# A two-layer decoder on one core: its planner prices PE's turns between parts of the array, and three groups of instructions become single pieces

## The chip, the cores and the metric

The kernel runs on one core of a Trainium2 chip. The metric is the time of one execution in microseconds (us) on the device; several executions are timed and their median is given. One more execution was taken by the hardware profiler. The engines are called PE (TensorE, matrix products and transposes), DVE (VectorE), ACT (ScalarE), POOL (GpSimd) and SP (the queue that starts most transfers).

## The reference

The input x has 128 sequences of 64 tokens with 128 features, all float32; ctx has the same shape. Two layers follow each other, each with three parts that are added to x after a layer norm:

```python
x = x + L0_attn(ln(x))            # 16 heads of 8, scores times exp(-|decay| * distance), softmax
x = x + L0_xattn(ln(x), ctx, mask)# 16 query heads on 4 key heads of 8, causal and padding mask, norm, Wo
x = x + L0_ffn(ln(x))             # 8 experts, top 2, at most 256 slots an expert are needed here
x = x + L1_attn(ln(x))            # 16 heads of 64, rotary embedding, causal softmax
x = x + L1_xattn(ln(x), ctx)      # bidirectional attention, four parts through W_l
x = x + L1_ffn(ln(x))             # 8 experts, top 1, hidden 512, gelu
```

## The kernel before

The 8192 tokens are cut into 16 supertiles of 512 tokens, each of four tiles of 128 tokens (two sequences a tile). X stays on the chip for the whole program. There are three phases, and each is recorded first and issued afterwards. Phase one walks the 16 supertiles through the first layer's self-attention, cross-attention and routing, and then the eight experts. Phase two walks them through the second layer's two attentions and its routing. Phase three runs 23 blocks of 512 rows through the second mixture of experts.

**The recorder and the planner.** `Loom` records every call as an `Op`: its engine, the views that it reads and writes, and an estimated cost (`effort`). Matmuls that follow each other into the same tile are joined into one op up to a cost of 1.29; `burst()` joins everything inside it into one PE op. An op is issued whole. Each recorded op gets a due time: its supertile's number times a period (`PER0`, `PER_E`, `PER1`, `PER2`) plus a phase from a list (`PHASES0`, `PHASES_E`, `PHASES1`, `PHASES2`), one entry for each op of a supertile. `plan()` sorts each engine's ops by due time and issues in that order; across engines it picks the op that could start first by its own clock of costs, and gives tiles their buffers and banks of PSUM on the way. So the phases set each engine's order, and the costs set which buffer a tile gets and how the engines' streams stand to each other. The planner already has a model of PE's clock (half rate after a window with little work), of the time in which instructions are fetched, and of the loading of activation tables. It has no term for PE going from one part of its array to another.

**Where the change sits.** Matmuls use the whole array of 128 rows by 128 columns or a part of it: the profile shows that as rows*columns. In phase one, `scores8` (L841, 32*64) makes scores, DVE scales or masks them (L930, L957) and takes the maximum (L847), POOL subtracts it (L848), `mixed8` transposes (L858, 128*128) and takes the exponential on ACT (L859), and then multiplies with the values (L868, 128*32) and with ones for the denominators (L875, 128*32); DVE divides (L879, L880). For each of the two tiles t of a call, `mixed8` records three PE ops: L868 for each of two sequences b and L875 once. L938 projects the output; L963 to L972 are the norm after cross-attention, L974 its variance on DVE. L804, L812 and L823 make queries, keys and values, L670 transposes the normed input.

In phase two, L1101 makes rotated queries and keys (DVE L1106, POOL L1109), L1120 the values, `scores64` the scores (L1136, 32*64) in one burst of 16 matmuls for each pair of tile t and head group m, and then for each of two halves i:

```python
for r in range(16):
    l.scalar.activation(rws[:, r, :], rws[:, r, :], AF.Exp, bias=mx[:, r:r + 1])
```

These 16 exponentials (L1146) are 16 separate ops of ACT, each with a due time of its own, so that other work of ACT may be put between them. `mixed64` transposes (L1160), copies (ACT L1161), multiplies with the values (L1169, 64*64), copies (ACT L1172, tile ots) and projects (L1175). The cross-attention after it has L1219, L1229, L1231, the transposes L1249, their copy on ACT (L1251, tile aT), L1262, L1270 and L1277.

Of the kernel before, what the change touches and what calls it, by code (L numbers as in the profile page):

```python
# [20 lines left out]
P = 128  # L21
S = 64
# [33 lines left out]
    17.44, -7.67, -0.70, 53.45, 48.54, 54.04, 45.63, 64.44, 88.63, 76.70, 85.96, 92.76, 172.77, 172.81, 162.05,  # L56
    172.78, 213.44, 234.93, 252.99, 269.10, 251.77, 267.83, 275.66, 267.71, 272.94, 257.68, 279.82, 278.83, 282.38,
    290.67, 293.04, 295.12, 295.46, 292.99, 296.71, 298.01, 298.42, 295.71, 298.60, 321.52, 295.79, 317.71, 306.66,
    305.94, 302.79, 303.43, 299.74, 301.78, 315.30, 316.81, 303.50, 329.32, 300.88, 323.27, 313.42, 317.58, 311.21,
    304.81, 305.08, 309.92, 317.64, 318.35, 306.20, 319.41, 320.24, 224.77, 252.61, 284.62, 298.75, 298.46, 297.40,  # L60
    299.11, 295.06, 316.85, 317.41, 276.24, 277.47, 325.19, 321.67, 321.86, 321.61, 327.96, 323.61, 323.96, 325.67,
    321.37, 324.49, 325.17, 327.24, 343.90, 347.34, 345.14, 340.60, 333.26, 348.22, 333.77, 355.36, 335.28, 342.90,
    343.98, 342.86, 343.43, 344.55, 346.09, 339.00, 351.60, 353.97, 347.01, 351.89, 354.86, 349.07, 349.93, 369.59,
    355.36, 373.48, 360.29, 369.71, 358.54, 368.69, 368.31, 359.10, 359.75, 368.64, 359.10, 373.88, 359.44, 374.41,
    371.20, 361.71, 361.46, 368.84, 366.56, 364.57, 368.59, 368.66, 373.75, 372.93, 386.89, 373.33, 373.42, 376.38,
    374.65, 377.76, 378.07, 377.78, 377.83, 382.39, 378.61, 382.46, 378.24, 382.5, 384.48, 384.54, 383.63, 381.68,
    379.30, 382.10, 386.18, 409.43, 406.59, 406.95, 406.30, 388.81, 391.65, 411.79, 398.09, 398.67, 401.96, 402.84,
    400.64, 403.77, 408.24, 408.65, 401.03, 408.25, 410.28, 411.47, 411.72, 415.13, 410.22, 415.89, 417.95, 419.56,
    444.39, 417.49, 417.41, 402.57, 428.64, 430.52, 432.99, 427.77, 437.23, 426.02, 434.32, 428.63, 434.83, 435.45,
    433.68, 436.02, 437.13, 438.02, 435.47, 434.08, 440.62, 439.70, 440.59, 455.31, 451.94, 447.95]  # L70
PHASES_E = [
    105.53, 216.96, 215.15, 217.11, 217.09, 217.12, 215.52, 107.48, 109.15, 176.01, 219.45, 106.60, 106.75, 175.45,
    217.56, 110.30, 223.67, 207.78, 222.32, 207.78]
PHASES1 = [
    -20.46, 145.81, 193.06, 195.35, 190.35, 171.30, 213.16, 200.50, 220.31, 210.13, 269.78, 283.10, 283.77, 297.78,
    320.65, 312.95, 304.84, 307.46, 338.28, 356.60, 362.19, 357.00, 356.94, 376.04, 344.33, 342.81, 342.61, 365.87,
    364.14, 359.49, 359.01, 380.76, 359.61, 354.22, 354.32, 372.13, 367.75, 361.90, 361.55, 381.69, 375.74, 371.74,
    371.82, 386.79, 381.12, 376.55, 376.18, 393.17, 384.39, 383.56, 391.73, 396.69, 439.67, 396.26, 403.73, 407.54,
    400.11, 396.37, 397.66, 402.37, 398.95, 397.16, 406.48, 430.61, 428.34, 428.16, 425.48, 414.54, 413.96, 420.18,
    429.59, 415.08, 415.07, 430.54, 427.36, 416.03, 422.46, 420.81, 425.31, 420.28, 422.64, 438.57, 398.93, 406.93,  # L80
    428.19, 419.49, 421.08, 417.61, 420.05, 420.04, 425.44, 426.95, 423.91, 437.89, 435.04, 424.61, 421.20, 420.57,
    429.88, 429.72, 421.62, 425.18, 438.82, 425.42, 427.01, 436.31, 436.67, 447.61, 441.7, 455.56, 445.97, 448.47,
    448.42, 413.95, 425.06, 432.86, 435.50, 446.42, 443.68, 466.58, 455.91, 464.02, 456.37, 434.04, 430.56, 429.21,
    429.77, 429.50, 431.19, 430.81, 427.54, 427.18, 429.84, 463.30, 465.33, 459.12, 458.15, 453.17, 466.35, 461.44,
    461.75, 461.06, 461.50, 465.34, 453.43, 449.87, 465.70, 465.01, 452.34, 450.68, 450.88, 457.41, 427.85, 428.57,
    454.82, 461.54, 458.53, 460.45, 462.36, 460.59, 448.56, 459.39, 453.92, 456.75, 455.84, 450.57, 461.14, 449.79,
    451.31, 463.76, 449.52, 449.54, 453.67, 442.24, 441.88, 458.89, 462.62, 466.97, 466.67, 467.98, 469.81, 470.19,
    464.54, 442.43, 442.93, 464.75, 464.67, 467.68, 469.90, 476.72, 470.79, 471.75, 465.75, 424.77, 432.67, 461.49,
    463.46, 466.01, 466.26, 465.36, 466.99, 467.10, 467.15, 485.07, 482.06, 485.04, 488.89, 495.16, 495.96, 489.08,
    496.00, 484.32, 496.66, 497.12, 486.51, 481.07, 499.30, 498.28, 499.42, 497.73, 490.36, 481.95, 482.47, 494.00,  # L90
    484.87, 486.64, 488.98, 511.36, 496.17, 497.35, 498.24, 491.71, 500.93, 499.07, 500.86, 492.13, 506.66, 497.31,
    505.28, 504.50, 495.57, 504.35, 509.70, 515.94, 506.02, 516.41, 506.09, 508.35, 509.21, 508.68, 511.88, 510.84,
    513.64, 510.15, 520.41, 516.91, 523.53, 527.86, 532.29, 533.30, 530.00, 532.06, 525.14, 536.09, 527.96, 521.61,
    523.47, 524.76, 524.75, 522.83, 528.14, 527.96, 526.58, 526.98, 529.26, 542.38, 530.39, 503.68, 533.08, 533.33,
    531.50, 544.83, 534.17, 540.35, 534.65, 537.12, 539.29, 540.66, 541.37, 539.43, 543.70, 545.67, 547.09, 548.20,
    551.06, 553.93, 548.17, 544.84, 552.03, 546.78, 559.80, 561.39, 559.95, 556.15]
# [128 lines left out]
class Op:  # L225
    def __init__(self, index, engine, table):
        self.index, self.engine, self.table = index, engine, table
        self.runs, self.uses, self.into = [], [], None
        self.cost, self.delay, self.count = 0.0, 0.0, 0
        self.needs, self.then, self.waits, self.ready = set(), [], 0, 0.0  # L230
        self.rows = False
# [53 lines left out]
class Loom:  # L285
# [13 lines left out]
    @contextmanager  # L299
    def burst(self):  # L300

        self.bursting = Op(len(self.ops), "PE", None)
        self._add(self.bursting)
        yield
        self.bursting = None
# [16 lines left out]
    def op(self, engine, run, reads, writes, cost, delay=0.05, tables=(), table=None, count=0):  # L322
# [14 lines left out]
        op.rows = engine == "POOL" and bool(tables)  # L337
        op.delay = delay
# [24 lines left out]
    def plan(self):  # L363
# [5 lines left out]
        loaded, count, since, clock = None, 0, 0.0, Clock()  # L369
        order = []  # L370
        while len(order) < len(self.ops):
            best = None
            for e, ops in queues.items():
                for op in ops[:1] if e != "SP" else ops[:40]:
# [3 lines left out]
                    if op.table is not None and op.table != loaded:  # L378
                        t += 1.3
                    if op.count and count + op.count > BLOCK:  # L380
                        t = max(t, since + FETCH)
# [29 lines left out]
            busy[op.engine] = op.many or op.rows  # L411
            end = free[op.engine] + op.delay
# [20 lines left out]
WINDOW, LITTLE = 3.413, 1.5  # L433

# [10 lines left out]
class Recorder:  # L445
# [5 lines left out]
    def __getattr__(self, what):  # L451
        def record(*a, **k):
# [11 lines left out]
            cost, delay = effort(self.engine, what, out, (*a, *k.values()))  # L464
            table = next((x for x in a if isinstance(x, AF) and x in (AF.Exp, AF.Silu, AF.Gelu)), None) if self.engine == "ACT" else None
            count = 0 if self.engine != "PE" else 2 if what == "transpose" else 4
            self.loom.op(self.engine, run, ins, [out] if isinstance(out, View) else [], cost, delay, table=table, count=count)
# [14 lines left out]
def effort(engine, what, out, args):  # L482
# [4 lines left out]
    if engine == "PE":  # L487
        passes = 1 if what == "transpose" else 2
        rows, cols = aps[0].shape[0], out.shape[0]
        share = 1  # L490
        for k in (rows, cols):
            share *= next(x for x in (32, 64, 128) if k <= x) / P
        return passes * max(0.008, (max(cols, n) * 0.00084 + 0.003) * share * 1.02), 0.38
# [22 lines left out]
def decoder_kernel(ctx: ExitStack, tc: tile.TileContext, x, cx, mask, consts, cols, rows, wa, wffn, wouts,  # L516
# [214 lines left out]
    with ExitStack() as ph:  # L731
# [119 lines left out]
        def mixed8(oT, pt, vbd, u):  # L851
# [9 lines left out]
            for t in range(2):  # L861
                pts = both[:, t]
                for b in range(2):
                    h = slice(b * S, (b + 1) * S)
                    with l.burst():
# [6 lines left out]
                with l.burst():  # L872
# [195 lines left out]
    with ExitStack() as ph:  # L1068
# [56 lines left out]
        def scores64(u, qr, kr):  # L1125

            scs = [ps.tile([P, 2, 2, 4, S], F32, name="sc") for i in range(2)]
            for t in range(2):
                for m in range(4):
                    with l.burst():  # L1130
                        for o in range(2):
                            for h in range(4):
                                for b in range(2):
                                    k0 = (2 * u + t) * P + b * S
                                    r = slice(32 * h, 32 * h + 32)
                                    l.tensor.matmul(scs[h // 2][b * S:(b + 1) * S, h % 2, t, m, :], lhsT=qr[r, m, o, k0:k0 + S],  # L1136
                                                    rhs=kr[r, m, o, k0:k0 + S], start=(o == 0), stop=(o == 1))
            pts = []
            for i in range(2):
# [5 lines left out]
                for r in range(16):  # L1145
                    l.scalar.activation(rws[:, r, :], rws[:, r, :], AF.Exp, bias=mx[:, r:r + 1])  # L1146
# [325 lines left out]
```

## Time and profile before

| what | value |
|---|---|
| median of 6 runs | 2085.39 us (2081.73 to 2088.47) |
| profiled execution | 2076.73 us, its span 2075.0 us |
| mean granted PE clock | 0.936 |
| busy share: PE, DVE, ACT, POOL | 87%, 66%, 51%, 63% |
| first layer's attentions | about 0 to 782 us |
| its experts and the way to the second layer | about 782 to 876 us |
| second layer's attentions | about 876 to 1866 us |
| second mixture of experts | about 1866 to 2075 us |

A line of a timeline has the start and the length in us, the engine, the source line, the operation, what it writes and reads, shapes, the count of equal instructions that were merged, and in brackets the idle time of the engine before it with what ended that wait. For PE the shape rows*columns is the part of the array. Each float32 matmul of the program stands as two records, each transpose as one. A list of windows gives for each stretch the busy time and count of PE, PEld (weight loads), DVE, ACT and POOL, the granted PE clock, the share of DMA engines busy, and GB/s.

### The profile page before, as it was taken

Reading aid. Unit: us, or ns where it says so; the run is one execution under the profiler, and the core shown is the slowest. Engines: PE = TensorE matmul, PEld = TensorE weight load, DVE = VectorE, ACT = ScalarE, POOL = GpSimd, SP = SyncE. Lnnn points to the kernel's source line nnn. Section 1 sums busy time; section 2 is a strip of 40 time slices with the busy share of each in tenths; the row PEclk is TensorE's granted clock in tenths of the full one; section 3 lists DMA queues with packets and bytes.
Section 4 is the critical chain, followed back from the end, with each engine's and each line's share of the span. In section 5 each row is a group of like instructions: output and inputs, shape, how many; then the busy total and the mean of one; then the engine's idle time right before and its main releaser. Section 6 shows DMA issues by size and latency. Waiting matters only on the chain. (4 is left out here: it accounts for less than half of the span.)

```text
span 2075.0 us, 67398 instructions
## 1 busy us (share of the span) xinstructions
PE 1798.0 (87%) x29088; PEld 1272.6 (61%) x29088; DVE 1374.2 (66%) x3425; ACT 1054.7 (51%) x2353; POOL 1309.1 (63%) x1184
## 2 busy tenths in 40 slices
PE   5788888888888873489999999999999999839997
PEld 3556566566565652346766766666666666637776
DVE  4767777787777763397777778788777777432222
ACT  5545555455545431136666656676566666613332
POOL 4446667677666665586676676776666666324665
PEclk9988999899999876799999999999999999969999
DMA  3311121111103000601011110100000000014441
GB/s 105 111 45 56 53 58 40 30 36 53 31 25 111 2 2 20 144 12 18 13 28 28 28 28 18 28 22 16 18 15 18 17 18 18 12 62 152 169 170 49
DMA packets 96690, 97.55 MB, mean 47 GB/s; under 512 B 19564, under 2 KB 82372, under 8 KB 96264
## 3 DMA queue, kind: packets, MB, share of 16 engines
q1 hardware_dynamic: 77848, 56.37, 9.3%
q0 software_dynamic: 18544, 36.87, 6.7%
q8 instruction: 228, 3.74, 0.8%
q14 instruction: 70, 0.57, 0.1%
HBM read 56.73 MB, written 45.81 MB: 49 GB/s over the span
## 5 line engine op out<-in xcount | busy, mean ns | idle before, releaser
L1106 DVE TENSOR_TENSOR hv<-ps,cst 128x1024 f32<-128x1024 f32 x256 | 304.8, 1214 | 43.7 <-PE ps L1101 41.1
L1109 POOL TENSOR_TENSOR rot<-hv 128x1024 f32<-128x1024 f32 x128 | 307.3, 2445 | 19.6 <-DVE hv L1106 14.4
L848 POOL TENSOR_TENSOR pt<-pt,mx 128x2048 f32<-128x2048 f32 x64 | 231.9, 3624 | 76.1 <-DVE mx L847 41.6
L1146 ACT ACTIVATE pt<-pt,mx 128x64 f32<-128x64 f32 x1024 | 269.6, 337 | 4.4 <-DVE mx L1144 4.4
L1101 PE MATMUL ps<-xT,w 128*128 128x512 f32 x512 | 252.0, 619 | 7.4 <-ACT ots L1172 6.8
L859 ACT ACTIVATE pts<-ps 128x1024 f32<-128x1024 f32 x128 | 130.4, 1022 | 128.0 <-PE ps L858 100.1
L815 ACT ACTIVATE km<-ps,kb,cst 128x512 f32<-128x512 f32 x128 | 95.7, 779 | 155.9 <-PE ps L670 76.4
L659 POOL TENSOR_SCALAR rs<-mv 128x4 f32<-128x4 f32 x96 | 22.0, 229 | 229.3 <-DVE mv L655 219.8
L638 POOL DMA_INDIRECT xin<-r,slots x128 | 129.7, 1013 | 38.9 <-issue 32.4
L1161 ACT COPY pts<-ps 128x1024 f32<-128x1024 f32 x64 | 64.8, 1014 | 171.4 <-PE ps L1160 170.3
L858 PE MATMUL ps<-ident,pt 128*128 128x128 f32 x1024 | 141.8, 286 | 10.7 <-POOL pt L848 7.4
L1175 PE MATMUL ps<-wo,ots 128*128 128x128 f32 x1024 | 143.3, 284 | 4.0 <-ACT ots L1172 3.5
L847 DVE TENSOR_REDUCE mx<-pt 128x32 f32<-128x2048 f32 x64 | 145.3, 2271 | 0.1
L1175 PEld LDWEIGHTS ps<-wo,ots 128*128 128x128 f32 x1024 | 125.4, 192 | 28.1 <-issue 14.4
L663 ACT ACTIVATE xn<-X,nb,rs 128x128 f32<-128x128 f32 x256 | 114.7, 485 | 53.2 <-POOL nb L661 30.9
L1101 PEld LDWEIGHTS ps<-xT,w 128*128 128x128 f32 x512 | 89.6, 193 | 82.7 <-issue 68.0
L1120 PE MATMUL ps<-w,xT 128*64 128x512 f32 x512 | 134.2, 602 | 0.7 <-DVE hv L1106 0.7
L858 PEld LDWEIGHTS ps<-ident,pt 128*128 128x128 f32 x1024 | 115.5, 146 | 28.5 <-issue 12.3
L1150 POOL TENSOR_TENSOR pt<-pt,den 128x1024 f32<-128x1024 f32 x64 | 120.7, 1907 | 15.7 <-DVE den L1149 12.0
L879 DVE RECIPROCAL rd<-ps 128x256 f32<-128x256 f32 x64 | 112.2, 1753 | 21.7 <-PE ps L868 17.4
L1368 ACT ACTIVATE hT<-ps,wt 128x512 f32<-128x512 f32 x92 | 61.0, 686 | 127.0 <-PE ps L1367 73.8
L1136 PEld LDWEIGHTS ps<-rot,rot 32*64 32x64 f32 x8192 | 96.6, 131 | 41.1 <-ACT vl L1122 12.9
(259 smaller groups left out, 4052.2 us busy)
## 6 DMA issues: line engine op xcount, KB each, us to landing
xsort<-none SPq DMA_DIRECT2D x23, 516.0 KB, 6.3
xe<-xsort SPq DMA_DIRECT2D x23, 516.0 KB, 3.5
ytk<-zero SPq DMA_DIRECT2D x16, 512.0 KB, 3.8
X<-ytk POOLq DMA_DIRECT2D x32, 256.0 KB, 4.7
X<-in_x SPq DMA_DIRECT2D x16, 256.0 KB, 4.8
c<-in_cx SPq DMA_DIRECT2D x16, 256.0 KB, 4.6
c<-in_cx SPq DMA_DIRECT2D x64, 64.0 KB, 2.3
mk<-in_mask SPq DMA_DIRECT2D x16, 128.0 KB, 2.8
```

Source lines behind the costliest of these rows:

```text
L638: i = nc.gpsimd.indirect_dma_start(out=dst, out_offset=bass.IndirectOffsetOnAxis(ap=index.real(), axis=0), in_=src.real(), in_offset=None, ...
L847: l.vector.tensor_reduce(mx, rws, AX.X, ALU.max)
L848: l.gpsimd.tensor_tensor(out=rws, in0=rws, in1=last(mx, S), op=ALU.subtract)
L858: l.tensor.transpose(tp[:, c, :], pt[:, c // 2, t, j0:j0 + 2].rearrange("p j k -> p (j k)"), ident)
L859: l.scalar.activation(both[:, t], tp, AF.Exp)
L1101: l.tensor.matmul(pp[:, h], lhsT=w1[:, qk, c * P:(c + 1) * P], rhs=xT, start=True, stop=True)
L1106: l.vector.tensor_tensor(hv[:, o].rearrange("p h (b s) -> p h b s", s=S), pp.rearrange("p h (b s) -> p h b s", s=S), tab.unsqueeze(2).to_b ...
L1109: l.gpsimd.tensor_tensor(out=r[:, m], in0=hv[:, :, 0], in1=hv[:, :, 1], op=ALU.add)
L1120: l.tensor.matmul(pv[par * S:(par + 1) * S, b], lhsT=xT[:, k0:k0 + S], rhs=w1[:, 2, par * NCH * S:(par + 1) * NCH * S], start=True, stop=True)
L1146: l.scalar.activation(rws[:, r, :], rws[:, r, :], AF.Exp, bias=mx[:, r:r + 1])
L1150: l.gpsimd.tensor_tensor(out=rws, in0=rws, in1=last(den, S), op=ALU.mult)
L1175: l.tensor.matmul(py, lhsT=ots[:, c // 4, c % 4, :], rhs=wo[:, c, :], start=(c == 0), stop=(c == NCH - 1))
```

## The change

The planner's ops get a field `part`, the rows and columns of the array that a PE op uses. When the next PE op has another part than the one before, its start is put 0.095 us after the end of the one before, at the least. The smallest cost of a matmul pass rises from 0.008 to 0.0085. `burst` takes an engine and an activation table. Three groups become single ops: in `mixed8` the L868 matmuls of both sequences and the L875 matmuls of a tile (24 matmuls, before three ops); in `scores64` the scores of two head groups (32 matmuls, before two ops of 16); and the 16 exponentials of a half (before 16 ops of ACT). The lists `PHASES0`, `PHASES_E` and `PHASES1` have new values, with fewer entries where ops were joined; the periods and `PHASES2` are as before. The matmuls and the other arithmetic are the same.

```diff
@@ Loom
-    def burst(self):
-        self.bursting = Op(len(self.ops), "PE", None)
+    def burst(self, engine="PE", table=None):
+        self.bursting = Op(len(self.ops), engine, table)
...
+        op.part = part
@@ plan
+                    if op.part != part and e == "PE":
+                        t = max(t, free[e] + CHANGE)
...
+            part = op.part if op.engine == "PE" else part
...
+CHANGE = 0.095
@@ Recorder
+            part = None
+            if self.engine == "PE":
+                part = next(x for x in (*a, *k.values()) if hasattr(x, "shape") and x is not out).shape[0], out.shape[0]
@@ effort
-        return passes * max(0.008, (max(cols, n) * 0.00084 + 0.003) * share * 1.02), 0.38
+        return passes * max(0.0085, (max(cols, n) * 0.00084 + 0.003) * share * 1.02), 0.38
@@ mixed8
-                for b in range(2):
-                    h = slice(b * S, (b + 1) * S)
-                    with l.burst():
+                with l.burst():
+                    for b in range(2):
+                        h = slice(b * S, (b + 1) * S)
                         for a in range(2):
                             for g in range(4):
                                 l.tensor.matmul(po[32 * g:32 * g + 32, 0, t, h],
...
-                with l.burst():
                     for a in range(2):
                         for g in range(4):
                             l.tensor.matmul(po[32 * g:32 * g + 32, 1, t, :],
@@ scores64
-                for m in range(4):
+                for i in range(2):
                     with l.burst():
-                        for o in range(2):
-                            for h in range(4):
-                                for b in range(2):
+                        for m, o, h, b in product((2 * i, 2 * i + 1), range(2), range(4), range(2)):
...
-                for r in range(16):
-                    l.scalar.activation(rws[:, r, :], rws[:, r, :], AF.Exp, bias=mx[:, r:r + 1])
+                with l.burst("ACT", AF.Exp):
+                    for r in range(16):
+                        l.scalar.activation(rws[:, r, :], rws[:, r, :], AF.Exp, bias=mx[:, r:r + 1])
@@ PHASES0, PHASES_E, PHASES1: all values new
```

## The prediction

> **What bounds the kernel now.** First the stretches: busy time per engine over windows cut at the stages (first layer's attention, its tail with the eight experts, second layer's ramp, steady part and end, the last mixture of experts). Columns: window, its length, then busy us of PE, PEld, DVE, ACT and POOL, granted clock, DMA share, GB/s.
>
> ```profile
> 136.10:426.70 290.60, 247.41 (x4224) 171.78 (x4225) 213.84 (x543) 147.37 (x241) 185.11 (x175) 0.88 0.17 48
> 426.70:737.90 311.20, 269.54 (x4879) 191.82 (x4878) 242.96 (x585) 159.84 (x255) 212.49 (x189) 0.94 0.14 38
> 737.90:874.20 136.30, 68.14 (x684) 49.86 (x683) 56.08 (x263) 23.39 (x48) 74.97 (x87) 0.71 0.25 55
> 976.30:1729.40 753.10, 739.18 (x13535) 512.56 (x13534) 581.57 (x1391) 476.30 (x1297) 523.01 (x435) 1.00 0.09 21
> ```
>
> The second layer (976 to 1729) is TensorE's: 98% busy at clock 1.00, a supertile every 57.8 us (start of L1231, from one to the next). The first layer is not: PE 85 to 87%, DVE 74 to 78%, each waiting for the other, at clock 0.88 and 0.94. The start of L938 comes 47.8 us apart in most of the first eight supertiles and 44.4 in the next five.
>
> Second, PE's timeline in the second layer: start, us, instruction, idle before it.
>
> ```profile
> 1209.46 0.38 PE L1249 MATMUL ps<-ident,a 128*128 128x128 f32 x2
> 1210.31 1.11 PE L1262 MATMUL ps<-aT,c 64*128 64x64 f32 x16 [0.46 <-ACT aT L1251]
> ...
> 1225.86 0.70 PE L1101 MATMUL ps<-xT,w 128*128 128x512 f32 x1 [0.51 <-ACT ots L1172]
> ...
> 1230.06 1.50 PE L1175 MATMUL ps<-wo,ots 128*128 128x128 f32 x12
> 1231.49 0.31 PE L1136 MATMUL ps<-rot,rot 32*64 32x64 f32 x8
> ...
> 1245.89 1.50 PE L1175 MATMUL ps<-wo,ots 128*128 128x128 f32 x12
> 1247.23 0.60 PE L670 MATMUL ps<-ident,r 128*128 128x128 f32 x4
> ```
>
> The same twelve matmuls of L1175 hold PE 1.34 us when the next tile has their part of the array (128*128) and 1.43 us when it is 32*64: entering another part costs 0.09. Leaving a small part costs about as much or more. In the first layer:
>
> ```profile
> 516.50 0.43 PE L868 MATMUL ps<-pts,vbd 128*32 128x64 f32 x16
> 516.75 0.62 PE L875 MATMUL ps<-pts,vone 128*32 128x128 f32 x16
> 517.18 0.41 PE L868 MATMUL ps<-pts,vbd 128*32 128x64 f32 x16
> 517.52 1.12 PE L841 MATMUL ps<-km,qT 32*64 32x256 f32 x32
> ...
> 521.09 1.80 PE L868 MATMUL ps<-pts,vbd 128*32 128x64 f32 x96 [0.82 <-DVE rd L879]
> 523.74 1.13 PE L812 MATMUL ps<-xT,w 128*128 128x512 f32 x2 [0.85 <-DVE oT L880]
> ```
>
> Sixteen of L868 take 0.25 us ahead of L875 (same part) and 0.34 ahead of L841 (another): 0.09 again. Elsewhere (553.37, L868 ahead of L858) it is 0.37 against 0.25, a surplus of 0.12; across the pairs of such rows it runs from 0.09 to 0.14, in a few 0.20. I take 0.11 us a turn, a middle of the common ones.
>
> Third, windows around the waits of the first layer show the clock:
>
> ```profile
> 284.70:289.30 4.60, 1.85 (x98) 1.47 (x97) 2.60 (x6) 3.92 (x7) 4.00 (x7) 1.00 0.03 5
> 289.30:292.80 3.50, 3.50 (x4) 1.11 (x4) 2.67 (x6) 0.00 (x0) 2.07 (x3) 0.51 0.02 6
> ...
> 528.50:531.70 3.20, 1.96 (x36) 1.01 (x36) 2.35 (x4) 0.00 (x0) 1.04 (x1) 1.00 0.01 3
> 531.70:535.10 3.40, 3.33 (x7) 1.51 (x6) 3.40 (x10) 2.03 (x4) 3.32 (x2) 0.50 0.01 0
> ```
>
> After a thin stretch (1.85 busy of 4.6 us) comes one of 3.4 us at half clock. A 47.8 us supertile has about 10.2 us at half clock, a 44.4 us one 3.4; the difference of the two periods is itself one such stretch.
>
> **The change, part by part.** All sums stand against the profiled execution, 2076.7 us (span 2075.0 and 1.7 around it); the median of the six runs is 2085.4, 8.7 higher, which I add at the end. No arithmetic is added or removed: both built programs have 15,646 matmuls. What moves is order, and the order of the built programs is known without a run.
>
> Turns. The changes of part on PE fall from 981 to 847: 496 to 368 in the first layer (32 to 23 a supertile, since L868 and L875 of one tile now stand in one piece of 24), 484 to 478 in the second (31 to 30; the scores, in pieces of 32 instead of 16, were mostly back to back already). So 128 x 0.11 = 14 us, and 6 x 0.11 = 0.7. A turn saved just ahead of a wait is worth nothing. PE's waits in a 44.4 us supertile (the list of waits, 515.5 to 560) sum to 5.5 us, 12%, so I take 88% of 14.7: **-13**. Bounds 0 (every saved turn lies ahead of a wait for DVE) and -18 (0.14 each).
>
> Two waits of the second layer. Now L1262 follows the transposes of L1249 at once and waits 0.46 for ScalarE's copy. In the new order eight matmuls of the output projection (0.22 each) and a pair of L1101 (1.72) stand between: 3.5 us of work over a copy that takes 0.37. It goes, with 0.53 us on PE: 15 x 0.53 = **-8**. L1101's 0.51 is for a bank that the copy ots frees, behind five exponentials. Whether that goes depends on ScalarE: between 0 and -8, I take **-4**.
>
> Exponentials in one piece. Before, 64 sets of 16 are cut up by copies; after, each set is one row of 16. Thirteen in a row took 3.21 us, so a set holds ScalarE 3.9 us, four sets a supertile. Behind each stand, in ScalarE's new queue, copies of ots, vl or pts, whose readers and whose banks' next users are PE's. ScalarE is 63% busy there and has one idle stretch of 8.9 us a supertile, so there is room to place the sets; whether each copy still comes in time the trace of before cannot show. Bounds: 0 for a set that meets slack, and 1.0 us on PE (twice the wait on ots above) for one that does not. I take **0**, the row nearest being L1146's own: 4.4 us of waiting in all, and PE's list of waits in a steady supertile having only the two named.
>
> Waits and clock of the first layer. The longest in a steady supertile are L841 on L974's chain (1.2), L875 and L868 on the reciprocal L879 (1.0 and 0.8), L812 on L880 (0.8). The new order takes L812 from between them and puts it behind the second scores, and the two pairs of L804, which stood together and followed a slow bank, now stand apart with scores and transposes between. The order L963, L967, L969, L972, L841 stays, so the 1.2 us wait and one half-clock stretch probably stay too. I take half a us a supertile, **-8**; bounds -40 (half of all 5.5 us, since DVE with 35 us of work in 44.4 cannot follow much closer) and +30 (a new wait of 1.9, the largest in these rows, in each).
> The early supertiles carry 6.8 us more at half clock, which costs half of it, 3.4, six times: 20 us. In the new build PE's order is the same from the third supertile to the thirteenth, and so it was before; what differed before was VectorE's and POOL's order. I take half: **-10**, bounds 0 and -20.
>
> On that clock the Trainium skill ("TensorE: Matmul & The Clock Gate", section "Why this matters for your kernels") says that matmul bursts keep the full rate as long as PE has no idle gap over about 3 us. The rows speak against it: half clock follows stretches whose longest wait is about 2 us. By the rule there would be no such loss to win back, and the sum would be 10 us smaller.
>
> Ramp, experts, end. The experts' order is new inside each expert (the next expert's transposes move ahead of L1049), but the stretch 738 to 874 is ruled by scatters, the DMA that brings rows back and one 22 us wait for the sums into X, none of which changes; the last stage keeps its phases. **0**, bounds -10 and +10: the phases put the second layer's first work elsewhere, and the 33 us ramp is all waits.
>
> Sum: -13 -8 -4 +0 -8 -10 = -43. 2076.7 - 43 = 2033.7, and with 8.7, **2042**.
>
> **The rivals.**
> ScalarE's pieces decide (slower). If each of the four sets delays a copy that PE needs by the upper bound of 1.0 us, the second layer loses 4 x 16 = 64 us against my 43: 2106. It decides from 43 / 64 = 0.67 us a set. For it: L1101 waits 0.51 already behind a run of only five. Against: the 8.9 us of idle ScalarE.
> The first layer stays at its period. If its waits and half-clock stretches take up the saved turns, as two periods one clock stretch apart suggest, only the 12 us of the second layer come: 2073.
> The first layer loses a clock stretch everywhere: 45.5 us on average falls to 41.0, 15 x 4.5 = 68, and the second layer wins its 12 to 16: about 2003. For it: 1.0 us of turns and 5.5 of waits to win; against: DVE's 35 us of work in strict turn.
> It does nothing: the turns fall, but new waits replace them one for one, 2085. The second layer's one turn in 31 shows how little a merged piece may do.
>
> **How the numbers follow.** Forecast 0.50 (2015 to 2065), first layer stuck 0.17, a stretch gone 0.13, nothing 0.05, ScalarE's pieces 0.15. A difference under 0.2% (4 us) can hardly be told from none here. Faster 0.80, same 0.05, slower 0.15. The range 2004 to 2088 takes in all but the pieces' case and half of the 2003 one.
>
> **What would show it.** Right: L1231 about 56.9 us apart instead of 57.8, L1262 without idle before it, clock 1.00 there; in the first layer L938 43 us apart and the clock above 0.93 from 136 on; L868 to L875 without a turn. Wrong: PE waiting for L1172, L1122 or L1161 in the second layer (pieces); a 44.4 us period kept with more waits on L879 (stuck); a longer gap between the last L1056 and the first L1101.

## The result, and the profile after

The changed kernel took 2091.8 us (median of 28 runs) against 2081.7 (65 runs) for the kernel before: ratio 1.0045, 95% interval 1.0033 to 1.0056, slower by 0.45%. In a later set it was 1.0056 (1.0036 to 1.0075). The prediction was 2042 us, 2004 to 2088, with 0.80 on faster. In three of the sets of experiments below the kernel before itself took 2230 us; ratios are therefore compared only inside a set.

The profiled execution after has a span of 2094.7 us, 19.7 longer than before; the medians are 10 apart, because the profiled execution before lies 5 us under its median (2076.7 against 2081.7) and the one after 5 us over (2096.7 against 2091.8). The shares that follow are of the 19.7. From first rows to first rows: the first layer, from its first L963 to its last (L965 after), fell from 683.2 to 659.9 us; from there to the first L1229 (L1230 after) it is 5.7 us longer; the second layer, from the first of these rows to the sixteenth, rose from 845.9 to 877.3; the end is 4.1 longer, the beginning 1.8. So -23 in the first layer, where about -30 was forecast, and +31 in the second, where -13 was.

First, windows of the profile after: first layer in two parts, then nine supertiles of the second layer and three later ones (columns as before: length, busy of PE, PEld, DVE, ACT, POOL, clock, DMA share, GB/s).

```profile
142.70:426.70 284.00, 244.83 (x4290) 175.28 (x4292) 219.86 (x551) 151.36 (x248) 192.43 (x182) 0.89 0.19 53
426.70:724.50 297.80, 253.29 (x4780) 186.32 (x4774) 234.72 (x573) 152.82 (x239) 202.10 (x182) 0.92 0.13 36
960.30:1514.40 554.10, 525.99 (x9363) 362.97 (x9363) 408.88 (x972) 330.41 (x900) 367.51 (x307) 0.97 0.10 21
1577.50:1751.00 173.50, 170.36 (x3126) 119.28 (x3124) 135.10 (x318) 110.22 (x301) 117.74 (x96) 1.00 0.06 16
```

The third row holds the work of nine supertiles (9,363 matmul records), for which the kernel before took 521 us (9,370 records from 976.1 to 1497.0, PE busy for 511.5, clock 1.00). Here it is 554, PE is 95% busy instead of 98%, and its clock is 0.97. The fourth row is back at 98% and 1.00. Between starts of L1230 the periods are 59.2, then 61.7 to 63.3 eight times, 59.3, and then 57.9, 57.7, 58.0: the loss has a beginning and an end.

Second, PE's waits in the second layer (total, times, longest), before from 976 to 1497 and after from 1019.7 to 1456.3:

```profile
PE ps L1101 <- ACT ots L1172: 4.7, 9, 0.5
PE ps L1262 <- ACT aT L1251: 4.1, 9, 0.5
```

```profile
PE ps L1230 <- DVE lim L1317: 20.6, 8, 2.6
PE ps L1122 <- ACT s L1266: 6.2, 7, 0.9
```

The two waits that the prediction wanted gone, L1262 for aT and L1101 for ots, are gone. Two others stand in their place. (Lines moved by one to three: L1230 is L1229 before, L1122, which makes the values, is L1120, and the copy L1266 is L1265.) The larger one in PE's timeline, and what DVE was doing:

```profile
1143.31 0.58 PE L1230 MATMUL ps<-ident,nmx 128*4 128x128 f32 x2 [2.57 <-DVE lim L1317]
1143.69 1.91 PE L1232 MATMUL ps<-xT,nwc 128*4 128x128 f32 x8
1145.53 2.37 PE L1103 MATMUL ps<-xT,w 128*128 128x512 f32 x4
```

```profile
1137.24 0.42 DVE L1223 TENSOR_REDUCE nmx<-ps 128x4 f32<-128x256 f32 x1
...
1143.00 0.17 DVE L1317 SCALAR_TENSOR_TENSOR lim<-ps,lim 128x8 f32<-128x8 f32 x1
```

L1230 multiplies nmx, which L1223 had ready at 1137.7. PE came to it at 1140.7 and started at 1143.3, at the end of L1317. L1317 updates the routing's limits and has nothing to do with nmx or with what L1230 writes.

Why it waits can be read in the build. The kernel's `BankPool` hands out single banks of PSUM, but what the program knows as a tile is a pair of banks, [128, 1024]. L1230 writes the tile pm in one bank of a pair; the other bank holds the routing's `board`, which L1317 reads. The program places waits by whole tile and by the order in which instructions were issued: an instruction waits for all that touched its pair and was issued earlier, whichever bank it was. In supertiles 2 to 10 of the changed build the last user of the other bank issued ahead of L1230 is L1317, in 11 to 15 it is L1302, some 3.5 us earlier on DVE; in the build before it is L1295 (L1296 after) in every steady supertile. That is one false wait (for work that the instruction doesn't need) in nine supertiles, and the trace shows it nine times.

The stall costs more than its 2.57 us, as three windows around it show:

```profile
1139.00:1143.30 4.30, 1.74 (x59) 1.45 (x49) 3.33 (x14) 3.90 (x7) 2.44 (x3) 0.96 0.06 10
1143.30:1146.70 3.40, 3.39 (x12) 1.81 (x13) 1.02 (x5) 0.22 (x1) 0.38 (x1) 0.55 0.50 70
1146.70:1151.00 4.30, 4.30 (x21) 2.65 (x20) 2.95 (x12) 1.50 (x6) 2.91 (x3) 1.00 0.15 55
```

With 1.74 us of work in 4.3, the next 3.4 us run at about half clock, 1.7 us lost. A period therefore adds up: 57.8 before, less 1.0 for the two waits gone, less 0.1 for one turn, plus 0.9 (L1122), plus 2.57 and 1.7, is 61.9; the trace has 61.7 to 63.3. Two further profiles of the changed kernel (in the second and fourth set below) have the wait nine times each. Three of these 18 waits are not followed by half clock, and their periods are 60.3 and 60.4 us: 1.6 less, the price of the half clock.

The Trainium skill ("TensorE: Matmul & The Clock Gate", section "Why this matters for your kernels") asks for no PE idle gap over about 3 us between bursts. The single gap here is 2.57 us, and the half clock comes after 24 of 27 of them all the same; the measurement decides.

### The profile page after: what moved, and what is told of

It is laid out like the page before. It is cut to its first block, busy times and chain, and to the rows that moved or that the text cites. A ratio compares the mean times of both kernels' runs of the same rounds, so it can differ in the third digit from the quotient of the medians.

```text
span 2094.7 us, 67469 instructions
## 1 busy us (share of the span) xinstructions
PE 1807.3 (86%) x29088; PEld 1288.7 (62%) x29088; DVE 1379.3 (66%) x3425; ACT 1058.3 (51%) x2353; POOL 1308.5 (62%) x1184
## 5 line engine op out<-in xcount | busy, mean ns | idle before, releaser
L1111 POOL TENSOR_TENSOR rot<-hv 128x1024 f32<-128x1024 f32 x128 | 302.1, 2368 | 48.8 <-DVE hv L1108 26.5
L1103 PE MATMUL ps<-xT,w 128*128 128x512 f32 x512 | 259.4, 639 | 0.7 <-ACT xT L1193 0.7
L1147 ACT ACTIVATE pt<-pt,mx 128x64 f32<-128x64 f32 x1024 | 251.2, 337 | 0.4 <-DVE mx L1144 0.4
L641 POOL DMA_INDIRECT xin<-r,slots x128 | 128.4, 1003 | 57.7 <-issue 30.6
L1122 PE MATMUL ps<-w,xT 128*64 128x512 f32 x512 | 140.3, 604 | 11.1 <-ACT s L1266 11.1
L1103 PEld LDWEIGHTS ps<-xT,w 128*128 128x128 f32 x512 | 94.4, 201 | 88.6 <-issue 80.5
L861 PEld LDWEIGHTS ps<-ident,pt 128*128 128x128 f32 x1024 | 112.7, 143 | 57.7 <-ACT pts L862 17.4
L850 DVE TENSOR_REDUCE mx<-pt 128x32 f32<-128x2048 f32 x64 | 145.4, 2271 | 0.1
L1136 PEld LDWEIGHTS ps<-rot,rot 32*64 32x64 f32 x8192 | 101.0, 131 | 44.2 <-issue 30.5
L881 DVE RECIPROCAL rd<-ps 128x256 f32<-128x256 f32 x64 | 111.5, 1747 | 19.7 <-ACT pts L862 7.1
L1136 PE MATMUL ps<-rot,rot 32*64 32x64 f32 x8192 | 116.3, 232 | 6.2 <-POOL rot L1111 4.0
```

Of the source, the lines that this page charges most:

```text
L641: i = nc.gpsimd.indirect_dma_start(out=dst, out_offset=bass.IndirectOffsetOnAxis(ap=index.real(), axis=0), in_=src.real(), in_offset=None, ...
L850: l.vector.tensor_reduce(mx, rws, AX.X, ALU.max)
L861: l.tensor.transpose(tp[:, c, :], pt[:, c // 2, t, j0:j0 + 2].rearrange("p j k -> p (j k)"), ident)
L1103: l.tensor.matmul(pp[:, h], lhsT=w1[:, qk, c * P:(c + 1) * P], rhs=xT, start=True, stop=True)
L1111: l.gpsimd.tensor_tensor(out=r[:, m], in0=hv[:, :, 0], in1=hv[:, :, 1], op=ALU.add)
L1122: l.tensor.matmul(pv[par * S:(par + 1) * S, b], lhsT=xT[:, k0:k0 + S], rhs=w1[:, 2, par * NCH * S:(par + 1) * NCH * S], start=True, stop=True)
```

## The experiments

**The first set: the false wait, and the two layers apart.** e1 moves nothing on any engine's queue; it only issues L1230 and L1232 as early as their inputs, the users of their own bank and PE's order allow, so that the routing's instructions come behind them in the program.

```diff
     def issue(self):
-        for op in self.plan():
+        order = self.plan()
+        for x in [op for op in order if op.early]:      # early: the op of L1230 and L1232
+            i, banks = order.index(x), {w.number for w in x.wholes if isinstance(w.kind, Banks)}
+            j = max(n for n, op in enumerate(order[:i]) if op.engine == "PE" or op in x.needs or any(
+                isinstance(w.kind, Banks) and w.number <= b < w.number + w.size for w in op.wholes for b in banks))
+            order.insert(j + 1, order.pop(i))
+        for op in order:
```

> The changed kernel with one thing moved: the op of L1230 and L1232 is issued as early among the other engines' instructions as its inputs, its own bank and PE's order allow. Every engine's own order and every bank stay as in the changed kernel. Theory (bank pair): L1230 waits 2.57 us for DVE's L1317 in nine supertiles because its bank is one half of a PSUM tile whose other half holds the routing's board, and the dependency covers the whole tile; a half-clock stretch of 3.4 us (1.7 us lost) follows. Then L1230 waits for nothing, the distance of L1232 falls from 62.0 to about 57.6 us in those nine, and the time falls by 9 x 4.3 = 38 us, from 2092 to about 2054. Rival (ScalarE's pieces): the exponentials of 3.9 us in one piece hold back what PE needs; then the distance stays at 62 or the wait moves to L1122, and the time stays within 6 us of 2092. Rival (DVE late): the second layer's DVE order is simply late; the wait moves to the next matmul that needs DVE and at most 10 us are won.

Measured: ratio 0.9674 (0.9604 to 0.9744), second layer 56.5 and then 57.6 to 58.1 us a supertile, no wait for L1317. The total, 2159.2 us, is 100 over what was expected, because the kernel before takes 2232.6 in this set.

e8 takes the counting out of the planner, with the new phases and pieces: all five engines' queues are then instruction by instruction those of the changed kernel, but L1302 stands ahead of L1230 in every steady supertile, and tiles get other banks.

```diff
-CHANGE = 0.095
+CHANGE = 0.0
-        return passes * max(0.0085, ...
+        return passes * max(0.008, ...
```

> The changed kernel with the planner's two numbers put back (CHANGE 0 instead of 0.095, 0.008 instead of 0.0085). Each engine's queue is the same, instruction by instruction, since it goes by due time; what differs is how the queues are merged and which bank a tile gets. In this merge L1302, not L1317, is the last use of the pair's other half ahead of L1230 in all steady supertiles. Bank pair: L1302 ends 0.9 us before PE gets there, so the wait goes, the distance is 57.5 to 58 throughout, 2050 to 2060. ScalarE's pieces or DVE late: the queues being the same, 2085 to 2095.

Measured: 0.9696 (0.9637 to 0.9756), 57.4 us a supertile, the total again 100 over. e4 has the changed second layer (phases, pieces) on the old first layer, e3 the opposite; both with the counting.

```diff
@@ e3: scores64 and its exponentials as before
-PHASES1 = [-39.87, 170.07, 251.9, 241.09,
+PHASES1 = [-20.46, 145.81, 193.06, 195.35,
...
@@ e4: mixed8 and PHASES_E as before
-PHASES0 = [-7.64, -13.14, -4.82, 13.52,
+PHASES0 = [17.44, -7.67, -0.70, 53.45,
...
```

> The reverse: PHASES0, PHASES_E and mixed8 as before the change; scores64, exponentials, PHASES1 and planner as changed. Bank pair: in this kernel too L1317 stands ahead of L1230's counterpart in nine supertiles, so 31 us are lost there and 3 at the end: 2115 to 2118. ScalarE's pieces: the same loss. If the first layer's gain and the second's loss depend on each other, nearer to 2082.

> The change in the first layer and the experts (PHASES0, PHASES_E, mixed8) and in the planner; scores64, the exponentials and PHASES1 as before the change. All theories that put the loss into the second layer expect its distance of 57.8 us back and the first layer's gain kept: 2081.7 - 21 + 5 for the experts, about 2065. If instead the first layer's gain is only time handed on to the second (its start is earlier, its end is not), 2080 to 2085.

Measured: e4 0.9975 (0.9934 to 1.0017), eight periods of 60.3 to 63.3 us, then 59.3, 57.9, 57.7, with the wait for L1317 nine times; e3 0.9924 (0.9889 to 0.9958), without that wait. The false wait goes with the new second layer, as expected; the ratio of 1.016 for e4 and the 57.8 us for e3 are missed. A reason for both is in e3, which has the old order in the second layer and there took 60 to 63 us a supertile, not 57.8 (PE's timeline):

```profile
1239.01 0.49 PE L1176 MATMUL ps<-pts,vl 64*64 64x64 f32 x14 [0.40 <-issue]
...
1245.00 0.35 PE L1143 MATMUL ps<-rot,rot 32*64 32x64 f32 x6 [0.39 <-issue]
1245.74 0.46 PE L1143 MATMUL ps<-rot,rot 32*64 32x64 f32 x18 [0.38 <-issue]
...
1247.66 3.50 PE L1108 MATMUL ps<-xT,w 128*128 128x512 f32 x4
```

PE stops inside bursts of its smallest matmuls, at about the same instruction of each supertile, and waits for nothing that the profile shows; the four matmuls after that take 3.50 us where 1.9 is usual. Over the second layer these stops come to 18 us in e3, and to 2 to 4 in the kernels with the new order there. In the first layer the three kernels of this set with the new order had 36 to 40 us of such stops between 200 and 700 us (e4, with the old order, 8.3), where the profile after of the first comparison has one of 0.7. So in this set the old second layer (896.5 us in e3) loses more than the new one does by its false wait (876.8 in e4), and the ratio of e4 says nothing against the loss. (The kernel before has no profile in this set; e3's second layer stands in for its own.) What stops PE the profile does not name, and e4's first layer, the longest of the set (788 us against 750 to 762), is not explained by its few stops.

**The second set: repeat, counting alone, turns, one set of exponentials.** Here the kernel before took 2080.5 us again.

> The changed kernel as it is, beside the others of this set, so that all stand on one chip. Theory (a wait for L1317 ahead of L1230 in nine supertiles): nine periods of about 62.0 us in the second layer and then 57.8, whatever the chip; total 1.0045 of the kernel before if the chip is like the one of the first comparison, 0.985 to 1.00 if it is like that of the first four experiments, where the kernel before itself loses 4 us a supertile in its second layer.

Measured 1.0056 (1.0036 to 1.0075), the same two waits, ten periods of 59 to 63 us: as expected.

e9 is the kernel before with the counting of turns and the new least cost, and nothing else.

```diff
+                    if op.part != part and e == "PE":
+                        t = max(t, free[e] + CHANGE)
...
+CHANGE = 0.095
...
-        return passes * max(0.008, ...
+        return passes * max(0.0085, ...
```

> The kernel before with the planner's counting of turns and nothing else: old phases, old pieces. The queue of each engine but SP's keeps its order, and L1302's counterpart, not L1317's, stands ahead of L1230. Theory: the counting by itself costs and brings nothing, ratio 0.998 to 1.002, second layer as before it. Rival (the counting itself makes the plan better): under 0.996. Rival (the counting always brings the false wait): 62 us periods and 1.01 or more.

Measured 1.0137 (1.0107 to 1.0167): all three readings missed. The second layer is as before, 57.8 us, with L1295's counterpart ahead of the bank's other user in every steady supertile. The loss is ahead of it: the first layer takes 704.6 us instead of 683.2, and the way to the second layer 5.8 more. Apart from two places on SP each engine's queue is the old one; what differs is banks and the order across engines. PE's waits from 150 to 740:

```profile
PE ps L877 <- DVE rd L888: 21.8, 17, 2.1
PE ps L850 <- DVE rs L983: 11.5, 11, 1.5
PE ps L679 <- ACT km L824: 10.1, 7, 1.4
...
PE ps L821 <- ACT km L824: 6.2, 3, 2.2
```

(L877, L888, L850, L679, L821 and L824 are L868, L879, L841, L670, L812 and L815 before.) Before, PE waited 14.3 us for the reciprocal at L868 and 13.1 at L875; here it is 21.8 and 1.0, so these waits moved and did not grow. The last row's wait of 2.2 is not in the list before. The larger part of the loss goes with the clock: in ten steady periods, 25 us longer than before, PE idles 10 us more and is busy 15 us more, and the clock records show 111 us at half clock instead of 68. e4, which has the same first layer, shows the same waits (2.09 for the reciprocal, 1.74 for km in one supertile), so its 0.9975 probably holds this loss too.

e10 is e1 with 98 neighbouring pairs of pieces in the first layer and 48 in the second cut in halves and interleaved (A1 B1 A2 B2), where no op between them needs the first.

```diff
+        for a, b in jobs:      # a, b: neighbours on PE with different parts
+            n, m = len(a.runs) // 4 * 2, len(b.runs) // 4 * 2
+            b.runs = b.runs[:m] + a.runs[n:] + b.runs[m:]
+            a.runs = a.runs[:n]
```

> The kernel with L1230 issued early (e1), in which pairs of neighbouring pieces of different parts are cut in halves and interleaved, so that the same matmuls make 196 turns more in the first layer (some 12 a supertile) and 96 more in the second (6 a supertile). Price of a turn in the prediction: 0.11 us, 88% of it in the first layer. Then the second layer's period goes from 57.6 to 58.2 and the first layer's grows by 1.2 us. Rival (turns cost nothing, the hardware overlaps them): 57.6 and no growth. Rival (0.2 a turn): 58.8 and 2.3.

Measured: ten first-layer periods take 473.0 us with 348 turns, against 453.1 with 230 in e11 of the same set: 0.17 us a turn. Ten second-layer periods take 593.1 with 350 against 577.0 with 290 in e1: 16.1 us, of which about 3.3 are two new waits for ACT (2.7 us in 480), and the rest 0.21 a turn (e1 is of another set, but both run at clock 1.00 there). Neither free nor 0.11; the rival of 0.2 is nearest. The whole kernel takes 2123.0 us, 1.0196 (1.0171 to 1.0221). A halved piece also hands over its result later, but PE's idle time in the ten first-layer periods is only 1.5 us more than in e11; 18.4 of the 20 us are busy time.

e11 is e1 with the one set of exponentials that stands ahead of the copy L1266 cut in 12 and 4, the copy between.

```diff
+            if b.late and len(a.runs) == 16:            # b: the copy c2q of L1266, a: the op ahead of it on ACT
+                a.runs, b.runs = a.runs[:12], b.runs + a.runs[12:]
```

What it takes apart, in the trace of the changed kernel: the copy that L1122's bank needs stands behind a set of 3.91 us on ACT.

```profile
1088.66 3.91 ACT L1147 ACTIVATE pt<-pt,mx 128x64 f32<-128x64 f32 x16
1092.47 0.56 ACT L1266 COPY s<-ps 128x512 f32<-128x512 f32 x1
```

```profile
1089.85 1.11 PE L1263 MATMUL ps<-aT,c 64*128 64x64 f32 x16
...
1093.09 1.94 PE L1122 MATMUL ps<-w,xT 128*64 128x512 f32 x8 [0.89 <-ACT s L1266]
```

> The kernel with L1230 issued early (e1), in which the set of 16 exponentials ahead of the copy s (L1266) is cut in 12 and 4 with the copy between, so that this one set is no longer one piece. Theory (the piece delays the copy, and PE waits 0.89 us for it ahead of L1122): that wait goes and the second layer's period falls from 57.6 to 56.7, 13 to 14 us in all against e1. Rival (the copy would be late anyway, or the bank is the last thing): 57.6.

Measured 0.9799 (0.9746 to 0.9852), 2045.0 us, against 2091.9 for the changed kernel in the same set. The second layer in its windows and at L1246 (L1230 in the changed kernel):

```profile
963.20:1516.00 552.80, 552.61 (x10090) 388.43 (x10090) 443.57 (x1056) 358.24 (x977) 399.10 (x333) 1.00 0.11 24
```

```profile
1076.75 0.38 PE L1246 MATMUL ps<-ident,nmx 128*4 128x128 f32 x2
...
1133.45 0.38 PE L1246 MATMUL ps<-ident,nmx 128*4 128x128 f32 x2
```

56.7 us apart, no wait before either, PE busy 552.6 of 552.8 us at clock 1.00: the second layer that the prediction had forecast (56.9). This version is faster than both kernels.

**The third set: all of PE early.** e8 and e1 once more, and two kernels that carry e1's idea to every PE instruction.

> The changed kernel without the planner's counting of turns (CHANGE 0 and the old least price of a matmul), on a chip in the state of the second set. Theory (the counting's only effect on the second layer is to put L1317 ahead of L1230): second layer 57.4 us a supertile, total about 33 us under the changed kernel, 0.988 of the kernel before; with e9 (counting alone, +30 us) this says that the counting costs some 30 us on the old phases and on the new. Rival (the phases and pieces cost the time, the counting helps): 1.005 or more.

> The changed kernel with nothing but L1230 issued early, on a chip in the state of the second set. Theory: second layer 57.6 us a supertile, clock 1.00 there, first layer as in the changed kernel; total 2058 us, 0.989. Rival (the stall hid something else that is now late): over 2075.

Measured 0.9688 (0.9630 to 0.9745) and 0.9665 (0.9615 to 0.9716) with the kernel before at 2230 us, so both totals are 100 us over what was expected; the periods, 57.4 and 57.6, are as expected.

```diff
+            if op.engine == "PE":      # others keep their place in the order
+                key[op] = max([before, *(key[x] for x in op.needs), *(last.get(b, -1.0) for b in banks)]) + 1e-4
```

> The kernel before with the counting alone (e9: 1.0137), in which each instruction of PE is issued as early as its inputs, the users of its own bank and PE's order allow, so that PE no longer waits for readers of the other bank of a pair. Theory (e9's 30 us are false waits of the same kind, in the first layer and the ramp): first layer back to 683 us or less from the first to the last L972 (e9: 705), total at or under the kernel before, 0.985 to 1.000. Rival (e9's loss is another assignment of banks, with true waits): 1.01 or more.

> The changed kernel with every PE instruction issued as early as it may be, as in e12, and the one set of exponentials cut in 12 and 4 around the copy s, as in e11 (0.980). Theory: the second layer keeps 56.7 us; in the first layer the waits of L673 and L871 for L881 (1.2 and 0.9 us) are of the same false kind and go, so its period falls from 44.3 to 42 or 43 us, total 2010 to 2030, 0.966 to 0.976. Rival (VectorE now waits for PE in the same pairs, or the waits are true ones): 44 us or more, total 2045 or above.

Measured 1.1033 (1.0975 to 1.1091) and 1.0602 (1.0545 to 1.0660): the rival held, and far beyond its number. The first layer of e14 is near 60 us a supertile, where e1 in this set takes about 51; the second is 60 to 64. DVE's list of waits from 200 to 700 in e14:

```profile
DVE X L956 <- PE ps L892: 68.8, 9, 8.6
```

The false wait has two ends. L956 reads one bank of a pair, and in the build L892, which writes the other bank, is issued just ahead of it. Where PE is issued first, DVE now waits for PE in the same pairs, up to 8.6 us at a time. So e12 can't tell which of e9's waits are false ones, and that stays open.

**The fourth set: e1 and e8 beside the changed kernel.**

> The changed kernel as it is, the yardstick of this set. Nine periods of 62 us in the second layer, whatever the state; 1.0045 to 1.0056 of the kernel before if that one takes 2080 us, 0.98 to 0.99 if it takes 2230.

> The changed kernel with L1230 issued early, beside the changed kernel itself. Theory: 31 to 38 us under the changed kernel, all of it in the second layer (57.6 us against 62 in nine supertiles). Rival (part of it is given back at the end or in the first layer): under 20 us.

> The changed kernel without the planner's counting, beside the changed kernel itself. Theory: second layer 57.4 us a supertile where the changed kernel has 62, total 30 to 40 us under the changed kernel. If PE waits for nothing visible in the first layer (as in the first set), both are longer by some 100 us, and the difference between the two stays. Rival (the counting helps the rest of the kernel by as much as it costs in the second layer): within 10 us of the changed kernel.

> The first layer and the experts of the changed kernel (phases, pieces, counting) with the second layer's phases and pieces of the kernel before. Theory: the first layer brings what the two traces show, 18 to 22 us from its end to its end, and the second layer keeps 57.8 us: ratio 0.990 to 0.994 if the kernel before takes 2080 us. Rival (the old second layer gets the false wait by the counting as well): 62 us periods and 1.00 or more.

Measured, again with the kernel before at 2231 us: changed kernel 2199.0 (0.9831, 0.9781 to 0.9880), e1 2159.4 (0.9681, 0.9629 to 0.9732), e8 2156.2 (0.9653, 0.9605 to 0.9701), e3 2207.6 (0.9891, 0.9842 to 0.9939). Taking away the one false wait wins 39.5 us by issuing one op early (e1) and 42.8 by the planner without counting (e8). In the profiles the second layer, first L1230 to last, is 876.2 us in the changed kernel, 840.5 in e1, 834.9 in e8. PE's waits from 1108 to 1860, the changed kernel and then e1:

```profile
PE ps L1230 <- DVE lim L1317: 23.1, 9, 2.6
PE ps L1122 <- ACT s L1266: 7.7, 9, 0.9
```

```profile
PE ps L1128 <- ACT pt L1153: 8.9, 10, 0.9
```

L1128 is L1122: the exponentials' wait stays in e1, as e11 said. e3's ratio of 0.989 says little of the first layer alone: its old second layer runs at 60 to 63 us in this set too, 894.9 us in all.

## Why the prediction was wrong, point by point

**What failed.** "What moves is order, and the order of the built programs is known without a run": that order was read engine by engine, and there L1230 stands where it should. The order across engines, which decides what an instruction waits for, was not read. In the built program L1230 waits for ACT and for the count that DVE reaches with L1317, where the old build's L1229 waits for ACT alone. That the waits of a steady supertile are "only the two named" was right of the trace before; the sum then put new waits of PE in the second layer at nothing, except behind ScalarE's pieces. The false wait, with its half clock, cost about 4.2 us in each of nine supertiles, 38 in all. With it and L1122's wait gone (e11) the second layer takes 824.5 us, 21 less than before and better than the -13 of the sum; with both it takes 877.3, 31 more. So the whole came to +20 in the profiles where -43 was forecast. e1 and e8 take the false wait away and win 40 us in the set that has all three.

**Exponentials in one piece, taken at 0, bound 1.0 us a set.** One set of four delays a copy that PE needs, by 0.89 us, once a supertile; the other three meet slack. The trace after has this wait thirteen times, 11 us. e11 cuts this one set, and the period falls by just that, 57.6 to 56.7. The rival "ScalarE's pieces" had the mechanism and the size a set, and was four times too large. The copies that it and the marks name (ots, vl and pts, L1172, L1122 and L1161 in the old lines) are in time in the steady supertiles. The late one, s, was not on the list, and that PE now waits at a line of the same number, L1122, is chance.

**The two waits of the second layer, -8 and -4.** Both went, L1101's in every supertile instead of half.

**Turns, -13.** The counts hold: 23 a supertile instead of 32. In ten steady periods (the third L963 to the thirteenth, L965 after) the first layer goes from 462.2 to 450.4 us. These periods, before and after:

```profile
196.04:658.25 462.21, 396.64 (x7042) 276.81 (x7041) 352.42 (x872) 242.07 (x393) 312.29 (x287) 0.93 0.16 46
```

```profile
191.15:641.58 450.43, 388.51 (x7036) 281.25 (x7037) 350.64 (x868) 241.74 (x389) 305.91 (x284) 0.91 0.17 46
```

PE is busy for 8.1 us less, although the clock is lower: its records show 85 us at half clock after and 68 before. From period to period, in both traces, one us at half clock adds 0.43 to 0.46 us of busy time, so the 17 us more hide 7 or 8 us of gain. Without them PE's work falls by about 1.6 us a period for nine turns, an estimate of 0.17 to 0.18 a turn, as e10's 0.17 says from the other side. So the price of 0.11 was too low, and the turns won about 16 us in these ten periods where the sum had 9.

**First-layer waits, -8, and half clock, -10.** In these ten periods PE idles 3.7 us less, and the half clock gives back 7 or 8. Over all fifteen periods (683.2 and 659.9 us) idle time falls by 1.3 us and time at half clock from 140 to 133. So of the 23 us won about 19 are less work on PE, with the same matmuls and fewer turns (12 in the sum), some 3 are the clock (10 in the sum) and 1 the waits (8 in the sum). That the first layer missed its forecast by only 7 us is luck: one term too small against two too large. The early periods were also read too evenly: of L938's first eight distances only three are 47.8 us. The waits changed their places (L871 and L673 wait for L881, L965 for L882) and nearly kept their sum.

**Ramp, experts, end, 0 with bounds of 10.** +5.7, +4.1 and +1.8 at the beginning, 11.6 together: just outside.

**The planner's counting**, the change's first part, was costed only through the turns it would save. It saves none: with it taken out (e8) every queue is the same, because due times alone sort them. All it does is to shift the planner's clocks, and with them the banks and the order across engines. On the new phases that put L1317 ahead of L1230, on the old ones (e9) it cost 30 us, most of it in the first layer and the ramp. The first is shown by e1 and e8; which of e9's new waits are false and which are for a bank is not.

## What to carry to other kernels

Where a program tracks dependences by tile, two unrelated buffers in one tile depend on each other, in the order in which they were issued; so read the waits of each instruction in the built program, not only the order on each engine, above all when a planner decides that order. Here it was best to mend the false wait at the one place where it stalls: issuing one op early won 40 us, issuing all of PE's early lost over 100, since the wait then falls on the other side. Tiles of one bank each, which would leave no pairs, were not tried. And a long run of small instructions in one piece should be asked, set by set, what stands behind it in its queue.

## What the runs showed of the hardware

A gap of 2.57 us was followed by 3 to 6 us at half clock in 24 of 27 cases, in three profiles of the changed kernel; in the other three the period is 60.3 or 60.4 us instead of about 62. Going from one part of PE's array to another cost about 0.17 us in the first layer, by turns taken away (an estimate) and by turns added, and 0.21 in the second by turns added. And the same program took about 2081 us in one comparison and one set and 2231 in three sets; the record gives one set of either kind the same chip number. In the sets at 2231 PE stopped inside bursts of matmuls of 32*64, 64*64 and 128*32, mostly for 0.3 to 0.5 us and sometimes for 1.1, 36 to 40 us of it in 500 of the new first layer, with DVE's, ACT's and POOL's instructions as long as ever. What holds PE up there the profile does not name. In the one of these sets that measures both, the changed kernel is 1.7% faster than the one before; elsewhere it is 0.5% slower.
